# Three key blocks per group, three score slots, one value bank and one product bank in a four-layer attention and convolution kernel

## The chip, the cores and the metric

The kernel runs on one core of a Trainium2 chip. The metric is the device time of one execution in microseconds, as a median of several runs. A core has five engines with a queue each: TensorE (PE in the profile, its weight loads are PEld), VectorE (DVE), ScalarE (ACT), GpSimd (POOL) and SyncE (SP, which only starts DMAs here). Each engine works through its own instructions in their order and waits for the others by semaphores. TensorE writes to PSUM alone, eight banks of 512 fp32 values per partition; VectorE and ScalarE take results out of it.

## The reference

The input x is (4, 256, 48, 48) in fp32; an image is 256 channels by 2304 positions. Four layers follow each other, each as x + layer(group norm of x):

```python
# layer 0: 8 heads of 64, keys and queries of each channel normed over positions
qkv = einsum('oc,bchw->bohw', w_qkv, x); q, k = l2norm(q), l2norm(k)
out = softmax(q^T k * 10) v ; return w_out out + b_out
# layer 1: max pool, blur, four small depthwise convolutions, sigmoid gate, x * gate
# layer 2: one more attention (64 channels, 2304 x 2304) and a batch norm over its output
# layer 3: squeeze-and-excite, 3x3 depthwise convolution, instance norm, leaky ReLU
```

The attention of layer 0 is most of the work: 4 images x 8 heads x 2304 x 2304 scores, and as many weights times values. Layer 2 adds one head per image.

## The kernel before

**Units and groups.** Two heads are worked on together, one in partitions 0 to 63, the other in 64 to 127 (a "pair"; four pairs p=0..3 per image b). A *unit* is 384 queries (`SL`) of one pair against all 2304 keys, which are 18 blocks of 128 (`JB`). A *group* is `G` = 2 blocks, so a unit has `NG` = 9 groups. A *phase* is the 6 units of one pair, 16 phases in all; then four phases of 3 units each are the attention of layer 2.

**One block.** `scores(u, j)` makes two matmuls, one per head, with 64 rows of the array each, into one score slot of two banks (`ps_sc`, two slots), and ScalarE takes the exponential of both (line 229) into a `pt` tile of 128 x 768. `weigh(u, j)` makes two matmuls with 64 columns of the array each (line 242), which add `v` times `pt` into the value bank `av` (`ps_av`, two banks, one in use per unit). In fp32 each matmul is two records in the profile. `add_up(u, g)` adds the `pt` tiles of a group into `acc`: VectorE does it itself (lines 252 and 262) or, for the groups in `PAIRED`, GpSimd adds the two tiles into `half` (line 259) and VectorE adds `half` later (line 255). Per unit that is 13 sums on VectorE and 4 on GpSimd.

**The end of a unit.** `total(u)` sums `acc` over partitions by two matmuls with ones (line 267) into a product bank and takes the reciprocal on VectorE (line 272, 2.56 us). `divide(u)` lets ScalarE check the total (line 279), multiplies `av` by the reciprocal on VectorE (line 282), and checks the reciprocal. Then two output products (line 441), each added to x by VectorE (lines 446 and 450).

**The product banks.** Everything that TensorE makes beside scores, values and convolutions goes to `pj_tile()`, two banks (`ps_pj`): totals, output products, the q, k and v products of the next pair in `project` (lines 397 and 409), products of layer 2, statistics of the norms. A q or k product is copied to SBUF by VectorE (line 401) and then squared in place by ScalarE for its norm (line 402), so its bank is held until both are done; a v product is copied by ScalarE (line 414).

**The order.** `attend` writes the order of TensorE, VectorE, ScalarE and GpSimd out by hand; nothing is moved until the last section. For each group t it issues the scores of t, the sums of t-1, what is due (`finish`), some steps of the phase's *lanes*, a total that is due, and the value products of t-1. Lanes are generators: `project` for the next pair, the group norm, `layer1` for the image before (in p=1 and p=2 of images 1 to 3, and in the first two phases of layer 2), `project2` and `w_stats`. Their steps ("ticks") are spread evenly over the groups of the phase but for the last three. `layer1` is mainly VectorE's: 81 taps over each image and channel half, three to a tick.

**The rest.** Before `attend` the group norm of image 0 and `project(0, ...)` for the first pair run alone ("the first projection"): for six chunks of 384 positions, q, k and v products. The chunks are loaded (line 370) two ahead into three buffers `xs` and scaled by VectorE one ahead (`normed`, line 374); the pair's weights `w` (line 365) have two buffers. All these loads stand in SP's queue. After `attend`, `w_stats` of the last image makes 12 products, each read by VectorE (line 675), and layer 3 follows: `before_conv` with 12 products per image read by ScalarE (line 815), and the convolutions (line 870) in score slots. There a scheduler orders the instructions.

Of the kernel before, what the change touches and what calls it, by code (L numbers as in the profile page):

```python
# [9 lines left out]
F32 = mybir.dt.float32  # L10
AF = mybir.ActivationFunctionType
# [3 lines left out]
P = 128  # L15
# [40 lines left out]
def _drain(gen):  # L56
    for _ in gen:
        pass
# [4 lines left out]

G = 2
NG = JB // G
PAIRED = (1, 3, 5, 7)
NCH = NSL
# [6 lines left out]
def usual_path(  # L74
# [7 lines left out]
    small = ctx.enter_context(tc.tile_pool(name="small", bufs=2))  # L82
    ps_sc = ctx.enter_context(tc.tile_pool(name="ps_sc", bufs=2, space=bass.MemoryType.PSUM))
    ps_av = ctx.enter_context(tc.tile_pool(name="ps_av", bufs=2, space=bass.MemoryType.PSUM))
    ps_pj = ctx.enter_context(tc.tile_pool(name="ps_pj", bufs=2, space=bass.MemoryType.PSUM))

# [121 lines left out]
    big = keep.enter_context(tc.tile_pool(name="big", bufs=2))  # L208
    wqp = main.enter_context(tc.tile_pool(name="wq", bufs=2))
    xsp = main.enter_context(tc.tile_pool(name="xs", bufs=3))  # L210
    op = main.enter_context(tc.tile_pool(name="o", bufs=2))
    ppool = main.enter_context(tc.tile_pool(name="pt", bufs=5))
    apool = main.enter_context(tc.tile_pool(name="acc", bufs=2))
# [33 lines left out]
    def add_up(u, g):  # L247

        pts = [u["pt"][j] for j in range(g * G, (g + 1) * G)]
        if g == 0:  # L250
            u["acc"] = apool.tile([P, 2, SL], F32, tag="acc", name="acc")
            nc.vector.tensor_add(u["acc"], pts[0], pts[1])  # L252
            return
        if u.get("half") is not None:
            nc.vector.tensor_add(u["acc"], u["acc"], u["half"])  # L255
            u["half"] = None
        if g in PAIRED:
            u["half"] = hpool.tile([P, 2, SL], F32, tag="half", name="half")
            nc.gpsimd.tensor_add(u["half"], pts[0], pts[1])  # L259
        else:  # L260
            for pt in pts:
                nc.vector.tensor_add(u["acc"], u["acc"], pt)  # L262

    def total(u):
        u["l"] = pj_tile()
        for h in range(2):
            nc.tensor.matmul(  # L267
                u["l"][h * D : (h + 1) * D, :SL], lhsT=ones, rhs=u["acc"][:, h, :],
                start=True, stop=True,
            )  # L270
        u["rinv"] = rpool.tile([P, SL], F32, tag="rinv", name="rinv")
        nc.vector.reciprocal(u["rinv"], u["l"][:, :SL])  # L272

    finished = {}

    def divide(u):
        i = u["i"]
        junk = rpool.tile([P, SL], F32, tag="junk", name="junk")
        nc.scalar.activation(
            junk, u["l"][:, :SL], AF.Identity, accum_out=checks[:, 0, i : i + 1]  # L280
        )
        nc.vector.tensor_mul(u["o"](), u["av"][:, :SL], u["rinv"])
        finished[u["b"]] = finished.get(u["b"], 0) + 1
        nc.scalar.activation(
            junk, u["rinv"], AF.Identity, accum_out=checks[:, 1, i : i + 1]
        )
# [18 lines left out]
    def attend(phases):  # L305
# [7 lines left out]
        def finish(t):  # L313
            for fn in due.pop(t, ()):
                fn()

        for t, (u, g, st) in enumerate(groups):
            for j in range(g * G, (g + 1) * G):
                scores(u, j)
            if prev is not None:  # L320
                add_up(*prev)
            finish(t)
            if st["gen"] is None:
# [4 lines left out]
            until = -(-st["total"] * st["at"] // (st["n"] - 3))  # L328
            while st["done"] < until and next(st["gen"], st) is not st:
                st["done"] += 1  # L330
            if st["at"] == st["n"] - 1:
                _drain(st["gen"])
            if t in sums:
                total(sums.pop(t))
            if prev is not None:
                pu, pg = prev
                for j in range(pg * G, (pg + 1) * G):
                    weigh(pu, j)
                if pg == NG - 1:
                    sums[t + 1] = pu  # L340
                    due.setdefault(t + 2, []).append(lambda pu=pu: divide(pu))
                    for i, fn in enumerate(pu["after"]):
                        due.setdefault(t + 3 + i, []).append(fn)
            prev = (u, g)
        pu, pg = prev
        add_up(pu, pg)
        for j in range(pg * G, (pg + 1) * G):
            weigh(pu, j)
        for t in sorted(due):
            finish(t)  # L350
# [9 lines left out]
    def project(b, norm, pair):  # L360
# [7 lines left out]
        def fetch(s):  # L368
            xs[s] = xsp.tile([P, NK, SL], F32, tag="xs", name="xs")
            nc.sync.dma_start(xs[s], xv[:, :, b, s * SL : (s + 1) * SL])  # L370
# [8 lines left out]
        fetch(0)  # L379
        fetch(1)  # L380
        q = big.tile([P, N], F32, tag="q", name="q")
# [6 lines left out]
        for s in range(NCH):  # L388
            cols = slice(s * SL, (s + 1) * SL)
            if s + 1 < NCH:  # L390
                normed(s + 1)
            if s + 2 < NCH:
                fetch(s + 2)
            for t, to in ((0, q), (1, kk)):
# [12 lines left out]
            for i in range(SL // P):  # L407
# [7 lines left out]
                v[:, j0 : j0 + SL // P, :].rearrange("p j d -> p (j d)"), ps[:, :SL]  # L415
            )
            yield
        n2 = small.tile([P, 2], F32, tag="n2", name="n2")
# [1331 lines left out]
```

## Time and profile before

| | us |
|---|---|
| median of 3 runs (4351.93 to 4355.94) | 4355.51 |
| the profiled execution | 4356.0 |
| its span, first to last instruction | 4354.3 |
| PE busy (94%) | 4078.9 |
| DVE busy (68%) | 2952.5 |
| ACT busy (43%) | 1857.8 |
| POOL busy (24%) | 1065.0 |
| scores, L223, busy | 1364.9 + 176.6 |
| values, L242, busy | 1322.7 + 192.1 |
| exponentials, L229, busy | 1473.7 |

A row of the timeline gives the start, the time taken, the engine, the line, the operation and its tiles (out<-in), and how many records it merges; in brackets, how long the engine was idle before and what ended that. Matmuls overlap in their pipeline, so a run of them is best measured from its start to the start of the next run. The clock column is the share of TensorE's full clock that was granted; it takes the values 1 and 0.5, and a mean lies between.

### The profile page before, as it was taken

To read this page: it belongs to the slowest core of one execution; us is meant where nothing else is said; L and a number is where in the kernel's file an instruction comes from. 1 tells how busy PE (TensorE), PEld (TensorE's weight loads), DVE (VectorE), ACT (ScalarE), POOL (GpSimd) and SP (SyncE) were. 2 spreads that over 40 slices of the span, in tenths; PEclk is the share of its full clock that TensorE was granted. 3 is DMA by queue.
4 is the path that set the end of the run, shared out by engine and by line. 5 is a ranking of instruction groups with operands and counts; after the bars stand their busy time and mean duration, and the time that the engine had idled before them with its cause. 6 is when DMAs were issued, how large, how long until landed. Compare 5 with 4: busy or idle time off the path is not lost.

```text
span 4354.3 us, 50890 instructions
## 1 busy us (share of the span) xinstructions
PE 4078.9 (94%) x19922; PEld 1805.3 (41%) x19922; DVE 2952.5 (68%) x3719; ACT 1857.8 (43%) x3054; POOL 1065.0 (24%) x632
## 2 busy tenths in 40 slices
PE   7999999999989999999899999998899978899997
PEld 4444444444433344444333444443334433444554
DVE  4555556556989865579898655798975699754222
ACT  3444444444444444444444444444444323343211
POOL 1222222222222322222323222223232221223231
PEclk9999999999999999999999999999999988997999
DMA  4000000000000000000000000000000000000000
GB/s 146 15 15 19 12 15 8 19 15 15 12 11 12 15 12 19 12 15 12 11 15 12 12 19 15 12 15 8 8 1 1 1 1 1 1 1 1 22 33 34
DMA packets 44330, 67.50 MB, mean 16 GB/s; under 512 B 4336, under 2 KB 42032, under 8 KB 42032
## 3 DMA queue, kind: packets, MB, share of 16 engines
q1 hardware_dynamic: 41216, 62.92, 4.7%
q8 instruction: 158, 2.59, 0.3%
q10 hardware_dynamic: 2864, 1.24, 0.1%
q14 instruction: 92, 0.75, 0.1%
HBM read 54.71 MB, written 9.44 MB: 15 GB/s over the span
## 4 chain that ended last, share of the span: by engine, by line
PE 68%; DVE 27%; issue 2%; ACT 2%; POOL 1%; DMA 0%; DVEq 0%; ACTq 0%; POOLq 0%
PE sc L223 24%; PE av L242 23%; DVE acc L262 7%; DVE l1acc L564 7%; PE sc L870 7%; PE pj L397 5%; PE pj L441 3%; PE pj L409 2%; DVE acc L255 2%; DVE rinv L272 2%; PE pj L267 1%; PE pj L663 1%; ACT pt L229 1%; DVE xs L374 1%; PE pj L641 1%
## 5 line engine op out<-in xcount | busy, mean ns | idle before, releaser
L229 ACT ACTIVATE pt<-sc 128x768 f32<-128x768 f32 x1944 | 1473.7, 808 | 1524.1 <-PE sc L223 1429.3
L259 POOL TENSOR_TENSOR half<-pt 128x768 f32<-128x768 f32 x432 | 852.7, 1974 | 2630.6 <-ACT pt L229 2317.2
L223 PE MATMUL sc<-q,k 64*128 64x384 f32 x6912 | 1364.9, 513 | 52.2 <-ACT pt L229 49.4
L242 PE MATMUL av<-pt,v 128*64 128x384 f32 x6912 | 1322.7, 503 | 0.0
L262 DVE TENSOR_TENSOR acc<-acc,pt 128x768 f32<-128x768 f32 x864 | 947.8, 1097 | 128.0 <-ACT pt L229 42.2
L223 PEld LDWEIGHTS sc<-q,k 64*128 64x128 f32 x6912 | 596.5, 187 | 811.3 <-ACT pt L229 304.9
L242 PEld LDWEIGHTS av<-pt,v 128*64 128x64 f32 x6912 | 433.5, 137 | 726.2 <-issue 714.4
L255 DVE TENSOR_TENSOR acc<-acc,half 128x768 f32<-128x768 f32 x432 | 416.4, 964 | 192.0 <-POOL half L259 191.2
L564 DVE SCALAR_TENSOR_TENSOR l1acc<-pd,grid,l1acc 128x256 f32<-128x256 f32 x640 | 347.2, 542 | 18.2
L272 DVE RECIPROCAL rinv<-pj 128x384 f32<-128x384 f32 x108 | 275.9, 2555 | 110.7 <-PE pj L267 110.6
L397 PE MATMUL pj<-xs,w 128*128 128x384 f32 x768 | 303.1, 520 | 40.2 <-issue 32.7
L870 PE MATMUL sc<-pad,diag 128*128 128x384 f32 x864 | 293.0, 499 | 4.5 <-ACT pad L851 4.5
L402 ACT ACTIVATE pj<-pj 128x384 f32<-128x384 f32 x192 | 91.2, 475 | 402.6 <-DVE q L401 266.1
L870 PEld LDWEIGHTS sc<-pad,diag 128*128 128x128 f32 x864 | 165.8, 194 | 130.0 <-issue 16.0
L397 PEld LDWEIGHTS pj<-xs,w 128*128 128x128 f32 x768 | 136.2, 193 | 186.0 <-issue 101.5
L441 PE MATMUL pj<-o,wo 128*128 128x384 f32 x384 | 175.8, 540 | 39.2 <-DVE x L450 16.5
L450 DVE TENSOR_TENSOR x<-pj,x 128x384 f32<-128x384 f32 x144 | 79.9, 555 | 170.1 <-PE pj L441 170.1
L223 PE MATMUL sc<-qv,kd 64*128 64x384 f32 x864 | 176.6, 527 | 19.1 <-ACT pt L229 19.1
L242 PE MATMUL av<-pt,qv 128*64 128x384 f32 x864 | 192.1, 534 | 0.0
L409 PE MATMUL pj<-w,xs 128*128 128x128 f32 x1152 | 152.8, 283 | 13.7 <-DVE x L450 12.2
L409 PEld LDWEIGHTS pj<-w,xs 128*128 128x128 f32 x1152 | 139.2, 193 | 60.2 <-issue 28.9
L252 DVE TENSOR_TENSOR acc<-pt 128x768 f32<-128x768 f32 x108 | 107.1, 992 | 45.4 <-ACT pt L229 45.1
(137 smaller groups left out, 2102.4 us busy)
## 6 DMA issues: line engine op xcount, KB each, us to landing
xs<-in_x_dram SPq DMA_DIRECT2D x96, 384.0 KB, 3.3
x<-in_x_dram SPq DMA_DIRECT2D x8, 1152.0 KB, 8.6
out_dram<-x SPq DMA_DIRECT2D x8, 1152.0 KB, 4.2
w<-in_wqkv_dram SPq DMA_DIRECT2D x32, 192.0 KB, 3.7
wo<-in_wout_dram ACTq DMA_DIRECT2D x1, 512.0 KB, 4.8
dw<-in_dww_dram ACTq DMA_DIRECT2D x1, 132.0 KB, 5.4
wph<-in_thphi_w_dram ACTq DMA_DIRECT2D x2, 64.0 KB, 4.6
Ww<-in_W_w_dram ACTq DMA_DIRECT2D x2, 64.0 KB, 5.3
```

The costliest lines, as they stand in the source:

```text
L223: nc.tensor.matmul(ps[:, h, :SL], lhsT=u["of"]["k"][r, j * P : (j + 1) * P], rhs=u["of"]["q"][r, u["qc"]], start=True, stop=True,)
L229: nc.scalar.activation(pt, ps[:, :, :SL], AF.Exp)
L242: nc.tensor.matmul(u["av"][r, :SL], lhsT=value(u, j, h), rhs=pt[:, h, :], start=j == 0, stop=j == JB - 1,)
L255: nc.vector.tensor_add(u["acc"], u["acc"], u["half"])
L259: nc.gpsimd.tensor_add(u["half"], pts[0], pts[1])
L262: nc.vector.tensor_add(u["acc"], u["acc"], pt)
L272: nc.vector.reciprocal(u["rinv"], u["l"][:, :SL])
L397: nc.tensor.matmul(ps[:, :SL], lhsT=w[:, k, t, :], rhs=xs[s][:, k, :], start=k == 0, stop=k == NK - 1,)
L409: nc.tensor.matmul(ps[:, i * P : (i + 1) * P], lhsT=xs[s][:, k, i * P : (i + 1) * P], rhs=w[:, k, 2, :], start=k == 0, stop=k == NK - 1,)
L441: nc.tensor.matmul(ps[:, :SL], lhsT=wo[:, p, k * P : (k + 1) * P], rhs=o, start=True, stop=True)
L564: nc.vector.scalar_tensor_tensor(acc, src, w, acc, ALU.mult, ALU.add)
L870: nc.tensor.matmul(ps[:, h, :SL].rearrange("p (r c) -> p r c", c=HW), lhsT=diag[:, k, t, :], rhs=pad[:, r0 + dr : r0 + dr + RS, dc : dc + HW],
```

## The change

Groups are three blocks (`G = 3`, six groups a unit); PSUM is cut as three score slots (six banks), one value bank and one product bank; `pt` has seven buffers instead of five. GpSimd adds the first two blocks of groups 1 to 4, and VectorE adds the third block of these groups and the older `half`. A new function `take` copies the value bank to SBUF on ScalarE as soon as the last value product of a unit is issued, and `divide` reads this copy. The check of the total moves from `divide` to `total`. In `attend`, a group gives the place ahead of its value products either to what is due or to one step of the lanes; other steps due in the group come after its value products. `project` has one weight buffer instead of two, two chunk buffers instead of three, loads one chunk ahead, and scales a chunk after the products of the one before it.

```diff
-G = 2
+G = 3
-PAIRED = (1, 3, 5, 7)
+PAIRED = (1, 2, 3, 4)
...
-    ps_sc = ctx.enter_context(tc.tile_pool(name="ps_sc", bufs=2, space=bass.MemoryType.PSUM))
-    ps_av = ctx.enter_context(tc.tile_pool(name="ps_av", bufs=2, space=bass.MemoryType.PSUM))
-    ps_pj = ctx.enter_context(tc.tile_pool(name="ps_pj", bufs=2, space=bass.MemoryType.PSUM))
+    ps_sc = ctx.enter_context(tc.tile_pool(name="ps_sc", bufs=3, space=bass.MemoryType.PSUM))
+    ps_av = ctx.enter_context(tc.tile_pool(name="ps_av", bufs=1, space=bass.MemoryType.PSUM))
+    ps_pj = ctx.enter_context(tc.tile_pool(name="ps_pj", bufs=1, space=bass.MemoryType.PSUM))
...
-    wqp = main.enter_context(tc.tile_pool(name="wq", bufs=2))
-    xsp = main.enter_context(tc.tile_pool(name="xs", bufs=3))
+    wqp = main.enter_context(tc.tile_pool(name="wq", bufs=1))
+    xsp = main.enter_context(tc.tile_pool(name="xs", bufs=2))
-    ppool = main.enter_context(tc.tile_pool(name="pt", bufs=5))
+    ppool = main.enter_context(tc.tile_pool(name="pt", bufs=7))
...
         pts = [u["pt"][j] for j in range(g * G, (g + 1) * G)]
+        half = u.pop("half", None)
+        if g in PAIRED:
+            u["half"] = hpool.tile([P, 2, SL], F32, tag="half", name="half")
+            nc.gpsimd.tensor_add(u["half"], pts[0], pts[1])
+            pts = pts[2:]
         if g == 0:
             u["acc"] = apool.tile([P, 2, SL], F32, tag="acc", name="acc")
             nc.vector.tensor_add(u["acc"], pts[0], pts[1])
-            return
-        if u.get("half") is not None:
-            nc.vector.tensor_add(u["acc"], u["acc"], u["half"])
-            u["half"] = None
-        if g in PAIRED:
-            u["half"] = hpool.tile([P, 2, SL], F32, tag="half", name="half")
-            nc.gpsimd.tensor_add(u["half"], pts[0], pts[1])
-        else:
-            for pt in pts:
-                nc.vector.tensor_add(u["acc"], u["acc"], pt)
+            pts = pts[2:]
+        if half is not None:
+            nc.vector.tensor_add(u["acc"], u["acc"], half)
+        for pt in pts:
+            nc.vector.tensor_add(u["acc"], u["acc"], pt)
...
         nc.vector.reciprocal(u["rinv"], u["l"][:, :SL])
+        i = u["i"]
+        junk = rpool.tile([P, SL], F32, tag="junk", name="junk")
+        nc.scalar.activation(
+            junk, u["l"][:, :SL], AF.Identity, accum_out=checks[:, 0, i : i + 1]
+        )
+
+    def take(u):
+        u["araw"] = rpool.tile([P, SL], F32, tag="araw", name="araw")
+        nc.scalar.copy(u["araw"], u["av"][:, :SL])
...
-        nc.scalar.activation(
-            junk, u["l"][:, :SL], AF.Identity, accum_out=checks[:, 0, i : i + 1]
-        )
-        nc.vector.tensor_mul(u["o"](), u["av"][:, :SL], u["rinv"])
+        nc.vector.tensor_mul(u["o"](), u["araw"], u["rinv"])
...
             if prev is not None:
                 add_up(*prev)
-            finish(t)
...
-            while st["done"] < until and next(st["gen"], st) is not st:
+            if t in due:
+                finish(t)
+            elif st["done"] < until and next(st["gen"], st) is not st:
                 st["done"] += 1
-            if st["at"] == st["n"] - 1:
-                _drain(st["gen"])
             if t in sums:
                 total(sums.pop(t))
...
                 if pg == NG - 1:
+                    take(pu)
                     sums[t + 1] = pu
...
+            while st["done"] < until and next(st["gen"], st) is not st:
+                st["done"] += 1
+            if st["at"] == st["n"] - 1:
+                _drain(st["gen"])
             prev = (u, g)
...
         fetch(0)
-        fetch(1)
...
             if s + 1 < NCH:
-                normed(s + 1)
-            if s + 2 < NCH:
-                fetch(s + 2)
+                fetch(s + 1)
...
+            if s + 1 < NCH:
+                normed(s + 1)
             yield
```

More of the change, by code (lines that the diff above doesn't have):

```diff
@@ L272, in total @@
         nc.vector.reciprocal(u["rinv"], u["l"][:, :SL])
-    finished = {}
-    def divide(u):
         i = u["i"]
@@ L281, in divide @@
         )
-        nc.vector.tensor_mul(u["o"](), u["av"][:, :SL], u["rinv"])
+    def take(u):
+        u["araw"] = rpool.tile([P, SL], F32, tag="araw", name="araw")
+        nc.scalar.copy(u["araw"], u["av"][:, :SL])
+    finished = {}
+    def divide(u):
+        i = u["i"]
+        junk = rpool.tile([P, SL], F32, tag="junk", name="junk")
+        nc.vector.tensor_mul(u["o"](), u["araw"], u["rinv"])
         finished[u["b"]] = finished.get(u["b"], 0) + 1
@@ L348, in attend @@
             weigh(pu, j)
+        take(pu)
         for t in sorted(due):
```

## The prediction

> **What bounds the kernel now.** I read the slices of the page first, then the timeline of TensorE alone in a calm stretch, then the busy times stage by stage, then single places in the timeline. The slices of the page:
>
> ```profile
> PE   7999999999989999999899999998899978899997
> DVE  4555556556989865579898655798975699754222
> PEclk9999999999999999999999999999999988997999
> ```
>
> TensorE is full nearly everywhere, but VectorE is full too in three double humps and once near the end. Those are the phases whose lanes carry `layer1`. Counting exponentials (108 to a phase of one head pair) gives the borders of the phases; busy times in some of them, columns length, PE, PEld, DVE, ACT, POOL, clock:
>
> ```profile
> 848.30:1047.80 199.50, 198.64 (x1034) 85.59 (x1032) 116.37 (x132) 98.00 (x163) 44.74 (x25) 1.00 0.05 15
> 1047.80:1274.70 226.90, 210.09 (x1046) 88.66 (x1044) 202.13 (x256) 102.64 (x177) 61.86 (x33) 0.96 0.05 13
> 1274.70:1509.70 235.00, 206.74 (x1032) 87.41 (x1030) 209.55 (x260) 102.63 (x176) 66.03 (x31) 0.96 0.05 13
> 3584.20:3752.60 168.40, 135.65 (x590) 61.30 (x588) 154.77 (x220) 50.17 (x80) 39.67 (x21) 0.85 0.00 1
> 3752.60:3868.40 115.80, 115.00 (x590) 52.81 (x588) 69.69 (x88) 44.14 (x67) 21.80 (x12) 1.00 0.00 1
> 3962.00:3975.00 13.00, 12.97 (x22) 5.90 (x22) 7.33 (x15) 0.62 (x2) 8.38 (x25) 0.50 0.00 0
> ```
>
> So ten head-pair phases (all of image 0, p=0 and p=3 of the others) last 197 to 200 us and are TensorE's, DVE 58%. Six (p=1, 2 of images 1 to 3) last 226 to 235 us with DVE 89% busy (202 of 227, 210 of 235) and TensorE no longer full: VectorE's. Of the four phases of the second attention, the first two (157 and 168 us) are VectorE's, the last two TensorE's. TensorE in a calm stretch:
>
> ```profile
> 1038.00 1.56 PE L223 MATMUL sc<-q,k 64*128 64x384 f32 x8
> 1039.49 1.51 PE L242 MATMUL av<-pt,v 128*64 128x384 f32 x8
> 1040.93 1.56 PE L223 MATMUL sc<-q,k 64*128 64x384 f32 x8
> 1042.42 1.51 PE L242 MATMUL av<-pt,v 128*64 128x384 f32 x8
> ```
>
> A score run of two blocks takes 1.49 us, a value run 1.44. In a value run the weight loads start 0.32 us apart, four steps, 1.29 us. The rest, 0.20 and 0.15 us, is paid at each change between the two shapes. This rebuilds a calm phase: 54 x 1.49 + 54 x 1.44 + 12 q/k products x 1.49 + 6 v products x 1.53 + 12 output products x 0.8 + 6 totals x 0.70 = 199 us, against 199.5.
>
> **What the Trainium skill says.** "TensorEngine Tiling (Array Packing)", Key Properties: changing the tiling mode drains the array. The trace agrees, with 0.35 us for a there and back. "TensorE: Matmul & The Clock Gate", Part 1: the clock is halved unless the array has been busy. The trace agrees, and adds that TensorE may be 99.8% busy (12.97 of 13.00 us, last row above) with 64-row products and stay at 0.50. "SBUF — State Buffer", Who interferes with whom: a VectorE instruction with two SBUF inputs and a GpSimd one that reads SBUF exclude each other. The trace agrees: below, two sums that take 2.02 us elsewhere take 3.43 beside a GpSimd sum, 1.41 lost.
>
> ```profile
> 1058.09 3.43 DVE L262 TENSOR_TENSOR acc<-acc,pt 128x768 f32<-128x768 f32 x2
> 1058.79 1.92 POOL L259 TENSOR_TENSOR half<-pt 128x768 f32<-128x768 f32 x1 [4.64 <-ACT pt L229]
> ```
>
> **The change, part by part.** The sum is made against the profiled execution, 4356.0 us (span 4354.3), 0.5 over the median of the runs.
>
> *Three blocks to a group.* A unit has 6 groups instead of 9, so 3 x 0.35 = 1.05 us less. 108 units would give 113 us. It counts only where TensorE sets the pace: 10 phases x 6 units x 1.05 = 63 us, and 6 units in the last two phases, 6.3 us. In VectorE's phases 0. VectorE's 13 sums and GpSimd's 4 in a unit stay as many. Inside a gap, output and projection products no longer follow each other (4 per phase, 0.09 us each, a shape change saved): 4 us back. The third score slot only makes room for three blocks; TensorE's idle at L223 is 52 us in all.
>
> *One bank for all products (`pj`).* A product must now wait until its forerunner is evacuated. The turn, from the prologue:
>
> ```profile
> 37.13 2.75 PE L397 MATMUL pj<-xs,w 128*128 128x384 f32 x8
> 38.62 0.56 DVE L401 COPY q<-pj 128x384 f32<-128x384 f32 x1 [2.41 <-PE pj L397]
> 39.27 0.47 ACT L402 ACTIVATE pj<-pj 128x384 f32<-128x384 f32 x1 [1.47 <-DVE q L401]
> 39.66 0.19 ACT L402 ACTIVATION_READ_ACCUMULATOR pj<-pj 128x1 f32 x1
> 39.91 1.60 PE L409 MATMUL pj<-w,xs 128*128 128x128 f32 x12
> ```
>
> q starts at 37.13 (its records are the first four of eight), is copied, squared in place, and its bank is free at 39.85: 2.8 to 2.9 us, where the product alone holds TensorE 1.49, so 1.36 lost if another follows at once. A v product: 39.91 to its copy at 41.55, 0.48, so 2.17, 0.64 lost. A product that VectorE alone evacuates: 1.49 + 0.56 + 0.05, 0.61 lost. In the order of the changed program a run of values (6 x 0.32 + 0.15 = 2.09 us) or of scores stands between most products, which covers the 1.36. Uncovered in TensorE's ten phases: q or k directly ahead of a total 14 times, v 9 times, second-attention products 4 times: 19 + 6 + 2 = 27 us. Net there: -63 + 4 + 27 = **-32 us**. The last two phases: 10 adjacent products x 0.61, and three totals with one value run before the next product (reciprocal 2.56, check 0.7, wait 0.3, less 2.09: 1.4 each), against -6.3: **+4**.
>
> *The same bank in VectorE's phases.* There TensorE waits at the bank until VectorE comes, and VectorE then has nothing queued if the next evacuation follows in its own order. In a head-pair phase the order shows four such places: q ahead of a total (square 0.7, total 0.7, latency 0.3: 1.7), a total ahead of k (check 0.7, product 1.7: 2.4), an output sum ahead of q (1.7), statistics (about 1): 7 us, less 1.5 in the stretches where TensorE leads. **+33** for six. None of this is in the trace of before: bounds -1.5 (all covered by `layer1` steps) and +12 a phase. For the second attention's two phases, some 3 and 6 places of 1 to 2.4 us: **+14**, bounds 0 and +28.
>
> *The first projection*, drained alone before any attention. Before: 20.46 (first product) to 49.58 (last square), 29.1 us for six chunks. After, each chunk is q, k, v in turn on one bank. At full clock 2 x 2.85 + 2.17 = 7.9 us, in all 5 x 7.9 + 5.7 = 45, +16. But the stage starts cold: the first loads are 0.64 us apart, and it became warm at 26 us after 5.5 us without a break. With breaks after every product TensorE works 2.6 of 4.2 us, so I take cold: q or k turn 4.2, v 3.8 (twice 0.128 a record, then 0.19, 0.48, 0.05), 5 x 12.2 + 8.4 = 69. **+40**, lower bound +16. Loads: one chunk ahead instead of two, 8 to 12 us for a load of 3.3 (page, part 6), hidden; if the x loads delay them, up to 5 us.
>
> *The end.* The 12 products for the statistics run 1.28 us apart (half clock); on one bank each takes 1.68 (product to evacuation) + 0.57 + 0.05 = 2.30: 11 x 1.02. The 12 before the first convolution, 1.25 apart: 1.75 + 0.67 + 0.05 = 2.47: 11 x 1.22. In the convolutions the order splits the remaining products into about 15 more insertions x 0.35. **+29**, bounds +10 (clock recovers) and +40.
>
> *At nothing.* `take`: 108 ScalarE copies x 0.48 = 52 us on an engine 49% busy in a calm phase (98 of 199.5). It waits for the last value product; behind it stand the next exponentials, which wait for scores later than that anyway. If ScalarE were late, the next value run has 2.1 us of scores ahead of it; the cover gone costs at most 0.5 x 108 us. The check of the total now waits on ScalarE behind the reciprocal, ahead of one group's exponentials, by some 0.5 us; the score slots absorb it. The product in `divide` now reads SBUF only: 0 to -0.1 us x 108, taken as 0. One weight buffer: the load (3.7 us) has over a group, 4.2 us, and the SP queue holds only the chunk load behind it.
>
> **Sum**: -32 + 4 + 33 + 14 + 40 + 29 = +88, **4444 us**.
>
> **The rivals.** (a) Milder: the prologue warms (-24) and the `layer1` steps cover VectorE's waits in its eight phases (-37): 4383. For it: the two are my least certain terms. Against: the listed places have nothing between them. Chance 0.22. (b) Worse: VectorE and TensorE fall into lockstep at the bank, 15 us instead of 6 a phase in eight phases: 4516. For it: the reciprocal holds the only bank 3.3 us in every unit. Chance 0.14. (c) **Faster**: GpSimd's sums collide less with VectorE. Place: the eight VectorE phases; price 1.42 us for each collision (sums of 1232 ns mean there, 958 in a calm phase), some 21 in a phase, 170 in all. Half of them gone is -120: 4324. It decides from 62 collisions (8 a phase) on, where 88 us are paid. For it: the GpSimd sum now waits for VectorE's use of the half before it, which could put it beside PSUM reads. Against: right behind that use VectorE has another two-input sum. Chance 0.10. (d) The terms cancel: 0.04. That the runs don't get longer is excluded: the order shows six matmuls in each.
>
> **The numbers.** Forecast 0.50, the rest as given. The range takes in (a) and most of (b): 4375 to 4505. About 0.2% (9 us) is what a measurement can tell from no change: faster 0.10, same 0.05, slower 0.85.
>
> **What would show it.** Score runs of 2.13 us and value runs of 2.09; calm phases of 196 to 197 us; first exponential at 93 us (69 if warm) instead of 53; VectorE phases of 230 to 242 us with new idle time of VectorE ahead of reciprocals and q/k copies; 2.3 us between the last products. I am wrong if VectorE's phases shrink, or if calm phases are longer than 199.5.

## The result and the profile after

The changed kernel takes 4419.61 us (median of four runs, 4415.05 to 4423.38) against 4354.71 us before: 1.0149 times the time, 95% interval 1.0132 to 1.0167. It is slower, by less than the 4444 forecast and well inside the range. The profiled execution took 4415.05 us with a span of 4413.3, so 59.0 us of span are to be placed.

The slices of the page after hardly differ from before:

```profile
PE   6999999999888999998889999988899867997997
DVE  3565566556888856578887555788865788562222
PEclk9999999999999999999999999999999878996999
```

The first slice is thinner (a longer first projection), and VectorE's humps are 8s where they had 9s: it is less full in phases that are as long as before. Stage by stage (columns as before: length, PE, PEld, DVE, ACT, POOL, clock, and the DMA share and rate):

```profile
853.60:1049.90 196.30, 193.14 (x1034) 88.39 (x1032) 115.75 (x132) 97.64 (x168) 56.20 (x25) 1.00 0.05 15
1049.90:1276.60 226.70, 201.45 (x1040) 92.27 (x1038) 190.63 (x255) 102.59 (x182) 66.66 (x32) 0.96 0.05 13
1276.60:1513.40 236.80, 204.46 (x1038) 92.99 (x1036) 199.84 (x260) 102.30 (x183) 73.04 (x33) 0.94 0.04 12
3580.90:3769.20 188.30, 136.91 (x594) 64.32 (x592) 153.48 (x222) 50.67 (x84) 47.12 (x23) 0.83 0.00 1
3980.00:4413.30 433.30, 375.96 (x1040) 195.26 (x1034) 110.58 (x206) 74.81 (x90) 111.31 (x99) 0.87 0.05 22
```

Row 1 is a calm phase, 3.2 us shorter. Rows 2 and 3 are VectorE's phases: their lengths are those of before (226.9 and 235.0) to within 2 us, but VectorE's busy time fell from 202.13 to 190.63 and from 209.55 to 199.84. Some 10 us of busy time went away and 11 us of idle time came. Row 4, the second phase of the second attention, is 19.9 us longer with the same work: all of it is idle time of VectorE. Row 5 is the end, 36.6 longer.

The runs of matmuls in the same calm phase, TensorE alone:

```profile
1039.70 2.21 PE L223 MATMUL sc<-q,k 64*128 64x384 f32 x12
1041.83 0.91 PE L451 MATMUL pj<-o,wo 128*128 128x384 f32 x2
1042.68 2.16 PE L242 MATMUL av<-pt,v 128*64 128x384 f32 x12
1044.76 2.21 PE L223 MATMUL sc<-q,k 64*128 64x384 f32 x12
```

Twelve records in place of eight: a score run lasts 2.13 us from start to start, a value run 2.08. The runs did get longer. The terms of the forecast beside what the trace shows:

| term | forecast | measured |
|---|---|---|
| ten phases that TensorE paces | -32 | -27.9 |
| VectorE's six phases of the first attention | +33 | +7.0 |
| first two phases of the second attention | +14 | 0.0 and +19.9 |
| its last two phases | +4 | +6.9 and -1.1 |
| first projection | +40 | +17.5 |
| the end | +29 | +36.6 |
| sum | +88 | +58.9 |

Two terms were much too large, and the question is why: did the bank cost VectorE's phases nothing, or did something give it back?

### The profile page after: what moved, and what is told of

It reads as the page before. It is cut to its first block, busy times and chain, and to the rows that moved or that the text cites. A ratio compares the mean times of both kernels' runs of the same rounds, so it can differ in the third digit from the quotient of the medians.

```text
span 4413.3 us, 51038 instructions
## 1 busy us (share of the span) xinstructions
PE 4010.0 (91%) x19922; PEld 1868.3 (42%) x19922; DVE 2889.6 (65%) x3719; ACT 1856.7 (42%) x3162; POOL 1228.9 (28%) x632
## 3 DMA queue, kind: packets, MB, share of 16 engines
q8 instruction: 158, 2.59, 0.2%
## 4 chain that ended last, share of the span: by engine, by line
PE 69%; DVE 25%; ACT 2%; issue 2%; POOL 2%; DMA 0%; DVEq 0%; ACTq 0%; POOLq 0%
PE sc L223 23%; PE av L242 22%; DVE l1acc L574 7%; PE sc L880 7%; PE pj L405 6%; DVE acc L262 5%; PE pj L451 3%; PE pj L417 3%; DVE acc L260 2%; DVE rinv L272 2%; PE pj L673 2%; PE pj L267 2%; POOL half L253 1%; DVE acc L257 1%; PE pj L651 1%
## 5 line engine op out<-in xcount | busy, mean ns | idle before, releaser
L229 ACT ACTIVATE pt<-sc 128x768 f32<-128x768 f32 x1944 | 1438.0, 811 | 806.5 <-PE sc L223 742.8
L253 POOL TENSOR_TENSOR half<-pt 128x768 f32<-128x768 f32 x432 | 1019.2, 2359 | 2419.0 <-DVE acc L260 1401.3
L223 PE MATMUL sc<-q,k 64*128 64x384 f32 x6912 | 1289.3, 506 | 17.6 <-ACT pt L229 16.1
L242 PE MATMUL av<-pt,v 128*64 128x384 f32 x6912 | 1249.7, 496 | 0.0
L262 DVE TENSOR_TENSOR acc<-acc,pt 128x768 f32<-128x768 f32 x864 | 886.9, 1027 | 97.8 <-ACT pt L229 23.8
L223 PEld LDWEIGHTS sc<-q,k 64*128 64x128 f32 x6912 | 625.7, 189 | 634.8 <-issue 272.9
L260 DVE TENSOR_TENSOR acc<-acc,half 128x768 f32<-128x768 f32 x432 | 415.0, 961 | 99.8 <-POOL half L253 98.9
L574 DVE SCALAR_TENSOR_TENSOR l1acc<-pd,grid,l1acc 128x256 f32<-128x256 f32 x640 | 380.7, 595 | 18.4
L275 ACT ACTIVATE junk<-pj 128x384 f32<-128x384 f32 x108 | 53.0, 491 | 431.9 <-DVE rinv L272 431.9
L409 DVE COPY q<-pj 128x384 f32<-128x384 f32 x96 | 53.4, 557 | 209.2 <-PE pj L405 209.2
L267 PE MATMUL pj<-acc,ones 128*64 128x384 f32 x432 | 99.0, 538 | 89.7 <-ACT pj L410 58.5
```

What stands on the lines that cost most here:

```text
L223: nc.tensor.matmul(ps[:, h, :SL], lhsT=u["of"]["k"][r, j * P : (j + 1) * P], rhs=u["of"]["q"][r, u["qc"]], start=True, stop=True,)
L229: nc.scalar.activation(pt, ps[:, :, :SL], AF.Exp)
L242: nc.tensor.matmul(u["av"][r, :SL], lhsT=value(u, j, h), rhs=pt[:, h, :], start=j == 0, stop=j == JB - 1,)
L260: nc.vector.tensor_add(u["acc"], u["acc"], half)
L574: nc.vector.scalar_tensor_tensor(acc, src, w, acc, ALU.mult, ALU.add)
```

## Experiments

All stage times come from one profiled execution each, with the borders at the same exponentials; stages of the same code differ by up to some 3 us between executions, in the second attention above all, where three phases together differ by 7.2 (467.7 after and 474.9 in run 1, the same code there). Edits shift the line numbers by a few. "Calm" is the sum of the ten phases of the first attention that TensorE paces, "VectorE's" that of the other six, "L2" the first three phases of the second attention, "rest" its last phase and the end.

| kernel | first projection | calm | VectorE's | L2 | rest | span |
|---|---|---|---|---|---|---|
| before | 53.4 | 1989.8 | 1384.3 | 440.9 | 485.9 | 4354.3 |
| after | 70.9 | 1961.9 | 1391.3 | 467.7 | 521.4 | 4413.3 |
| 1 two banks at the ends | 54.2 | 1961.5 | 1390.6 | 474.9 | 486.4 | 4367.5 |
| 2 no step at the total | 70.9 | 1941.8 | 1349.9 | 463.4 | 519.5 | 4345.5 |
| 3 two slots, three banks | 52.6 | 2153.7 | 1446.6 | 457.3 | 479.7 | 4590.0 |
| 4 before, one bank | 76.4 | 2061.2 | 1501.6 | 470.6 | 524.6 | 4634.5 |
| 5 second half buffer | 76.4 | 1960.9 | 1393.1 | 472.3 | 520.3 | 4423.0 |
| 6 after, no GpSimd sums | 73.8 | 1957.8 | 1376.1 | 467.4 | 519.9 | 4394.7 |
| 7 before, no GpSimd sums | 52.8 | 2000.4 | 1291.6 | 427.1 | 484.3 | 4256.2 |
| 8 both mends (1 and 2) | 54.5 | 1941.8 | 1350.5 | 463.5 | 485.5 | 4295.8 |
| 9 as 6, square from the copy | 63.6 | 1948.6 | 1372.9 | 467.9 | 519.9 | 4372.9 |
| 10 as 6, no step at the total | 70.9 | 1942.0 | 1341.7 | 458.6 | 518.3 | 4331.5 |
| 11 before, GpSimd in calm phases | 53.4 | 1990.0 | 1297.2 | 425.7 | 486.3 | 4252.6 |
| 12 change with mends | 53.3 | 1938.1 | 1350.0 | 460.4 | 485.4 | 4287.3 |

**1. Two banks at both ends.** Outside `attend` the value bank is free, so products there take it in turn with the product bank.

```diff
+    ends = {"on": True, "n": 0}
+
     def pj_tile():
+        if ends["on"]:
+            ends["n"] += 1
+            if ends["n"] % 2:
+                return ps_av.tile([P, 512], F32, tag="av", name="av")
...
+    ends["on"] = False
     attend(phases)
+    ends["on"] = True
```

> The changed kernel, but outside attention (first projection, second statistics, convolutions), where the value bank lies unused, products take the product bank and the value bank in turn. Theory (the single bank's turn is the whole cost of both ends): the first projection comes back from 70.9 to 53-55 us and the end from 433 to 397-405, all phases between unchanged within 1 us each, in all 4415 - 17.5 - 33 = 4365. Rival (the order of the new loop costs the ends: one chunk loaded ahead instead of two and norms after the products, and the split remaining products in the convolutions): the ends stay long, first projection 62 or more, end 420 or more, 4395 to 4415.

Measured: 4368.83 us, 1.0033 times before (1.0019 to 1.0048). The first projection is back to 54.2 us, last phase and end to 486.4 (before 485.9). The end alone takes 398.5 us (before 396.7). So the single bank's turn is the whole loss at both ends to within 2 us, which leaves next to nothing for the shallower loading and the new loop there. The products for the statistics, first in the changed kernel:

```profile
3983.94 1.65 PE L673 MATMUL pj<-y,Ww 64*128 64x384 f32 x2 [3.27 <-ACT junk L275]
3986.24 1.64 PE L673 MATMUL pj<-y,Ww 64*128 64x384 f32 x2 [0.66 <-DVE bst L685]
```

then with two banks:

```profile
3976.09 1.48 PE L679 MATMUL av<-y,Ww 64*128 64x384 f32 x2
3977.37 1.48 PE L679 MATMUL pj<-y,Ww 64*128 64x384 f32 x2
```

One bank: 2.30 us from product to product, with a wait of 0.66 for VectorE each time. Two banks: 1.28, no wait.

**2. No lane step in the group that holds a total.** The steps due there are taken in the unit's other five groups, so that no product stands next to a total.

```diff
-            elif st["done"] < until and next(st["gen"], st) is not st:
+            elif t not in sums and st["done"] < until and next(st["gen"], st) is not st:
                 st["done"] += 1
-            if t in sums:
+            summed = t in sums
+            if summed:
                 total(sums.pop(t))
...
-            while st["done"] < until and next(st["gen"], st) is not st:
+            while not summed and st["done"] < until and next(st["gen"], st) is not st:
                 st["done"] += 1
```

> The changed kernel, but in the one group of six that holds the total no lane step is taken (its share falls to the next groups), so no product stands next to a total. Theory (uncovered turns of the one bank cost some 27 us in TensorE's ten phases, and part of the 26 us in the second attention): calm phases shorter by 1.5 to 3 us each, the second attention's four phases shorter by 5 to 20 together, VectorE's phases within 2, in all 4415 - 25 - 12 = 4378 (4360 to 4395). Rival (the work that is pushed into five groups stands next to other products there, two steps in a gap, and waits for the bank just as long): 4410 to 4425, calm phases unchanged.

Measured: 4352.13 us, 0.9995 times before (0.9986 to 1.0004), more gain than expected. Calm phases fall by 20.1 in all, as forecast for uncovered turns. But VectorE's six phases fall by 41.4, where I expected next to nothing: the bank may have cost a good deal there after all, and the +7.0 of the table above would then be a balance. (The edit moves steps of `layer1` away from the total too, so that this run alone does not show that it was the bank.)

**3. Two score slots and three product banks.**

```diff
-    ps_sc = ctx.enter_context(tc.tile_pool(name="ps_sc", bufs=3, space=bass.MemoryType.PSUM))
+    ps_sc = ctx.enter_context(tc.tile_pool(name="ps_sc", bufs=2, space=bass.MemoryType.PSUM))
...
-    ps_pj = ctx.enter_context(tc.tile_pool(name="ps_pj", bufs=1, space=bass.MemoryType.PSUM))
+    ps_pj = ctx.enter_context(tc.tile_pool(name="ps_pj", bufs=3, space=bass.MemoryType.PSUM))
```

> The changed kernel, but two score slots and three product banks in place of three and one (value bank still one). Theory (the bank's turn costs both ends and the uncovered turns; the third slot is needed by three blocks): first projection 53-56 us, end 397-405, no wait of TensorE at the product bank; but the third score block of a group waits for the first exponential, some 0.3 to 0.6 us in each of 36 groups, so calm phases 206 to 216 us instead of 196; VectorE's phases 225 to 237; in all 4360 + 100 = 4460 (4400 to 4510). Rival (the third slot matters little, as TensorE's idle at the score line was 52 us in all before): calm phases 193 to 197 us, in all 4290 to 4340, faster than before.

Measured: 4593.23 us, 1.0554 times before (1.0537 to 1.0572). The ends are cured, but a calm phase takes 216.0 us, 19.6 more than after: 0.54 for each of its 36 groups. The waits of TensorE in a calm phase are one single line (total us, times, longest):

```profile
PE sc L223 <- ACT pt L229: 13.2, 36, 0.5
```

The third score block waits for the first exponential, once in every group. (These waits are 13.2 of the 19.6 us; the rest, 6.4, the waits do not show.) Three blocks need the third slot, and its two banks are what the products lost. The whole run is 83 us above the end of the range I expected: most calm phases lie at its edge (216), and VectorE's phases, at 239 to 245 us, above the 225 to 237 I had put down.

**4. The kernel before with one product bank.** Two blocks to a group as before; the check of the total moves into `total`, as in the change.

```diff
-    ps_pj = ctx.enter_context(tc.tile_pool(name="ps_pj", bufs=2, space=bass.MemoryType.PSUM))
+    ps_pj = ctx.enter_context(tc.tile_pool(name="ps_pj", bufs=1, space=bass.MemoryType.PSUM))
...
         nc.vector.reciprocal(u["rinv"], u["l"][:, :SL])
+        i = u["i"]
+        junk = rpool.tile([P, SL], F32, tag="junk", name="junk")
+        nc.scalar.activation(
+            junk, u["l"][:, :SL], AF.Identity, accum_out=checks[:, 0, i : i + 1]
+        )
...
```

> The kernel before (two blocks to a group, two score slots, two value banks) with one product bank instead of two; the check of the total moved to right behind the reciprocal as in the change, since it must be done before the bank is asked for again. Theory (the single bank costs both ends some 54 us, and costs TensorE's and VectorE's phases on its own, with no gain from longer runs): first projection +16 to +40, end +30 to +40, calm phases +2 to +6 each, since runs of two blocks (1.49 us) cover less of a turn of 1.36 to 2.4 us, second attention +25 to +60, VectorE's phases +1 to +10 each; in all 4355 + 130 = 4485 (4440 to 4540). Rival (in attention the one bank costs next to nothing and the loss is at the ends alone): 4405 to 4420. The same run tells whether VectorE's collisions with GpSimd fall with the bank alone (theory: yes, from 21-24 to about 15 in a VectorE phase) or with three blocks to a group (then they stay).

Measured: 4636.42 us, 1.065 times before (1.0632 to 1.0668), 150 us beyond what I expected. Calm phases lose 71 us in all, VectorE's 117. One of the latter:

```profile
1351.40:1606.10 254.70, 218.07 (x1034) 91.37 (x1032) 208.52 (x260) 101.93 (x176) 61.16 (x31) 0.91 0.04 12
```

VectorE's busy time is that of before (209.55); its idle time went from 25.5 to 46.2 us. So one bank, with the check moved, costs such a phase some 20 us. The second question of this run has a clear answer too. Taking for each VectorE instruction what it takes above the median of its kind, the excess in these phases is 28 to 33 us here and 29 to 35 before, but 19 to 24 after. If that excess is taken for collisions with GpSimd, they do not fall with the bank; they fall with the rest of the change, the new groups and their order of sums.

**5. A second buffer for GpSimd's half sum.** In the changed kernel a GpSimd sum and the VectorE sums around it stand like this:

```profile
1105.85 0.95 DVE L260 TENSOR_TENSOR acc<-acc,half 128x768 f32<-128x768 f32 x1
...
1106.90 0.96 DVE L262 TENSOR_TENSOR acc<-acc,pt 128x768 f32<-128x768 f32 x1
1106.94 2.59 POOL L253 TENSOR_TENSOR half<-pt 128x768 f32<-128x768 f32 x1 [2.71 <-DVE acc L260]
```

VectorE's use of the old half releases GpSimd 0.04 us after VectorE has begun its next sum. VectorE's sum takes its usual 0.96 us, GpSimd's 2.59 instead of 1.81. "SBUF — State Buffer", section "SBUF: two separate sides" of the Trainium skill, says that of the two the one that starts first holds the port for its whole instruction; the trace agrees. Before, it was VectorE that came second. I took this order for the cause of the missing +26 and undid it:

```diff
-    hpool = main.enter_context(tc.tile_pool(name="half", bufs=1))
+    hpool = main.enter_context(tc.tile_pool(name="half", bufs=2))
```

> The changed kernel with a second buffer for GpSimd's half sum, nothing else. Theory (in the changed order a GpSimd sum is released by VectorE's use of the half before it, so it begins just behind a VectorE sum that is already running, and GpSimd pays for the collision; that is why VectorE's phases grew 1.2 us each and not 5.5): with a second buffer GpSimd starts at its exponentials again, its sum takes 2.0 to 2.2 us instead of 2.44 to 2.49, VectorE's lost time in collisions goes back from 19-24 to 29-35 us a phase, and VectorE's six phases of the first attention get longer by 7 to 12 us each; calm phases unchanged; in all 4415 + 60 + 5 = 4480 (4450 to 4500). Rival (collisions fell because VectorE, waiting for the bank, is less often busy when GpSimd works): collisions and phases stay, 4410 to 4420.

Measured: 4426.23 us, 1.0169 times before (1.0152 to 1.0186). GpSimd in a phase of p=2, first after, then here (count; busy us, mean ns; idle before, by releaser):

```profile
L253 POOL TENSOR_TENSOR half<-pt 128x768 f32<-128x768 f32 x24 | 59.8, 2493 | 122.8 <-DVE acc L260 66.1 <-ACT pt L229 56.6
```

```profile
L253 POOL TENSOR_TENSOR half<-pt 128x768 f32<-128x768 f32 x23 | 51.3, 2235 | 119.8 <-ACT pt L229 101.3 <-DVE acc L260 18.5
```

The mechanism is there: GpSimd is released by the exponentials again, its sum is shorter, and VectorE's excess rises from 19 to 21.5 us (p=1) and from 23.5 to 29.5 (p=2). But the time did not follow: VectorE's six phases are 1.8 us longer together, not 42 to 72 (p=2 by 5.0, p=1 shorter by 3.2), while its idle time in the first phase of p=2 fell from 37.0 to 30.1 us. (Of the 9.7 us more in the span, 5.5 are in the first projection, see below, and 4.6 in the second attention, within the scatter there.) As an explanation of the time my theory fell: in the changed kernel, time that VectorE loses to GpSimd comes out of its waits, at least the 2 to 6 us a phase that this run adds.

**6 and 7. No GpSimd sums, with and without the change.** If collisions and bank hide each other, both have to be seen alone. VectorE makes all sums, 24 more in a phase.

```diff
-PAIRED = (1, 2, 3, 4)
+PAIRED = ()
```

(7 sets the same in the kernel before.)

> The changed kernel with all sums of exponentials on VectorE (24 more sums of 0.96 us in a phase), none on GpSimd, so no collisions. Theory (the bank costs VectorE's phases some 11 us each, which falling collisions hid): VectorE's phases 235 to 243 us; beside the next run, which is the same without the change, 8 to 14 us longer each; in all 4415 + 6 x 6 = 4450 (4430 to 4480). Rival (the bank costs VectorE's phases next to nothing): 226 to 230 us, no longer than in the next run by more than 2.

> The kernel before with all sums of exponentials on VectorE, none on GpSimd. VectorE's load is then 210.7 - 29.7 + 24 x 0.96 = 204 us and 219 - 34.5 + 23 = 207 us in its two kinds of phase, idle 22: phases of 224 to 231 us, calm phases 199 to 200; in all 4355 - 6 x 3 = 4337 (4315 to 4365). Both theories expect the same here; it is what the run before it is held against.

Measured, one execution each: 4396.71 and 4257.98 us. The same two VectorE phases with the change:

```profile
1050.90:1274.50 223.60, 202.87 (x1038) 93.30 (x1036) 195.38 (x278) 102.78 (x183) 10.62 (x9) 0.95 0.05 13
1274.50:1509.80 235.30, 204.01 (x1038) 93.02 (x1036) 203.07 (x285) 102.46 (x182) 10.82 (x7) 0.94 0.05 13
```

and without it:

```profile
1055.40:1269.30 213.90, 201.82 (x1038) 86.76 (x1036) 196.65 (x279) 102.92 (x176) 10.78 (x9) 0.98 0.05 14
1269.30:1485.10 215.80, 202.09 (x1038) 86.46 (x1036) 198.97 (x284) 102.45 (x176) 10.97 (x7) 0.98 0.05 14
```

Nearly the same work, but VectorE idles 28.2 and 32.2 us with one bank, 17.3 and 16.8 with two. Over the six phases the change costs 1376.1 - 1291.6 = **84.5 us** when no collisions cover it; 75.8 of them are idle time of VectorE. The waits tell which: summed over these phases, VectorE waits 58.0 us for q and k products (12.9 without the change) and 15.3 us for totals (4.8), and TensorE waits 125.4 us for the bank, behind the check, the sums into x or the squares, against 1.2 us behind a sum into x with two banks. The granted clock falls with these waits (0.95 and 0.94 in the rows, 0.98 without the change); how much of the 84.5 the slower products are is not separated.

GpSimd's sums cost the kernel before 1384.3 - 1291.6 = 92.7 us there, and the changed kernel only 1391.3 - 1376.1 = 15.2. 84.5 - 92.7 + 15.2 = 7.0; this holds by construction and is no check of its own, but it gives the sizes of the two terms behind the +7.0. The rival of run 6 is wrong, and the size in my theory (8 to 14 a phase) holds in p=1 (9 to 10) and is too small in p=2 (16 to 20).

In all, run 6 lies 53 us below what I had expected: its phases did not grow to 235 to 243 us. Run 7 lies 80 us below what I had expected, because I had added up durations of VectorE that overlap in part (208.6 us summed in the first phase, 196.65 busy) and taken its idle time as given, which fell from 25 to 17 us; only its calm phases are longer than before, by 10.6 us in all. A surprise beside it: in run 7, VectorE does 24 more sums in each of these phases and is *less* busy than before (198.97 against 209.55), since each GpSimd sum saved it one sum of 0.96 us (23 in a phase) and the excess over the usual durations was 29 to 35. Over the six phases this fall of the busy time is about half of the 92.7 us; the other half, 45.1, is idle time that went with the sums, and I have not taken it apart.

**8. Both mends.** The edits of 1 and 2 together.

> The changed kernel with both mends: two banks in turn outside attention, and no lane step in the group that holds the total. Theory (the costs lie in different places and add up): 4352 - 46 = 4306 (4300 to 4315), 1.1% faster than the kernel before. Rival (they share a cause): 4325 or more.

Measured: 4297.09 us, 0.9871 times before (0.9854 to 0.9887), 9 us better than expected. The two costs lie in different places and add up. Three blocks with one bank can beat the kernel before, if the bank is not asked for twice in a row.

**9 and 10. Which turns of the bank cost VectorE's phases?** Both start from run 6. 9 reads the squares from the copy in SBUF, so that a q or k product gives its bank back at VectorE's copy; 10 adds the edit of run 2.

```diff
+                junk = rpool.tile([P, SL], F32, tag="junk", name="junk")
                 nc.scalar.activation(
-                    ps[:, :SL], ps[:, :SL], AF.Square, accum_out=ss[:, t, s : s + 1]
+                    junk, to[:, cols], AF.Square, accum_out=ss[:, t, s : s + 1]
                 )
```

> The changed kernel without GpSimd sums (as the earlier run of that, 4396.7 us), and the squares of q and k read from the copies in SBUF instead of from the bank, so that a q or k product's turn of the bank ends at VectorE's copy, some 0.75 us earlier; 12 turns in a phase. Theory (VectorE's phases are paced by turns of the bank, of every kind): first projection shorter by about 8 us, VectorE's phases by 4 to 9 each, calm phases by 0 to 3, in all 4396.7 - 8 - 40 - 10 = 4340 (4320 to 4360). Rival (the turns that cost time there are those of the total, which holds the bank over the reciprocal and the check, and of the sums into x): VectorE's phases within 2 of 223.6 and 235.3, in all 4380 to 4390.

> The changed kernel without GpSimd sums (4396.7 us) and with no lane step in the group that holds the total. Theory (a good part of the 84 us that the bank costs VectorE's six phases comes from products next to a total): the phases of p=1 shorter by 2 to 5 us, those of p=2 by 8 to 12, calm phases by 2 each, in all 4396.7 - 40 - 20 - 6 = 4330 (4315 to 4350). Rival (the turns of q, k and the sums into x among themselves set them): VectorE's phases within 2 of the run without the mend, in all 4365 to 4380.

Measured, one execution each: 4374.85 and 4333.34 us. The shorter q and k turns take 10 us from the first projection (some 2.7 of it the clock, see below) and 9 from the calm phases, but only 3.2 from VectorE's six: my theory of "every turn" falls, the rival holds. Keeping steps away from the total takes 34.4, of which 28.9 in p=2 (10.0, 11.1, 7.8). TensorE's waits for the bank in the first phase of p=2, behind the check of the total and behind sums into x (total us, times, longest), first in run 6, then in run 10:

```profile
PE pj L417 <- ACT junk L275: 6.0, 1, 6.0
PE pj L405 <- ACT junk L275: 4.4, 1, 4.4
PE pj L405 <- DVE x L460: 3.4, 1, 3.4
```

```profile
PE pj L418 <- ACT junk L275: 0.2, 1, 0.2
PE pj L418 <- DVE x L461: 4.9, 2, 4.4
PE pj L406 <- DVE x L461: 3.9, 2, 3.5
```

In run 6 a v product waited 6.0 us until the check of the total had let go of the bank. In run 10 that is gone: 10.4 us behind the check fell to 0.2 in this phase, which is 10.0 us shorter, and 53.5 to 0.5 over all six. What is left is behind VectorE's sums into x (75.5 us over the six phases) and the squares (19.4). The remaining 1341.7 - 1291.6 = 50.1 us I have not taken apart by a run; that the bank, held until VectorE comes to these sums in its queue, is their cause is read from the waits only.

**11 and 12. Each scheme at the best found here.** Since GpSimd's sums help only where TensorE sets the pace, they stay there and go elsewhere.

```diff
-        if g in PAIRED:
+        if g in PAIRED and u["gp"]:
...
+        u["gp"] = b == 0 or p in (0, 3)
         return u
...
-            "b": ("l2", b),
+            "b": ("l2", b), "gp": b >= 2,
```

11 is the kernel before with this edit, 12 the change with this, both mends and the square from the copy.

> The kernel before, with GpSimd's sums left only in the phases that TensorE paces; in VectorE's eight phases VectorE makes them. Theory (in VectorE's phases the collisions cost the kernel before 13 to 19 us each; in calm phases the GpSimd sums save up to 3): the run without any GpSimd sums, 4258, less some 12 to 30 in the calm phases: 4240 (4225 to 4255). Rival (its gain came from elsewhere than VectorE's phases): above 4260.

> The changed kernel with two banks in turn outside attention, no step at the total, GpSimd's sums only in the phases that TensorE paces, and squares read from the copies. It is held against the run before it: three blocks with one bank against two blocks with two, each at its best here. Theory (calm phases are 5 us better with three blocks, VectorE's still 3 to 10 us worse for the bank): 4297 - 40 - 15 = 4242 (4225 to 4265), within 20 of the run before it. Rival (without the collisions the bank's cost comes out in full in VectorE's phases): 4270 or more, clearly behind it.

Measured: 11 takes 4251.47 us, as expected, **0.9768** times before (0.9755 to 0.9781); 12 takes 4289.00, 0.9851 (0.9836 to 0.9867). Three blocks are 51.9 us better in the calm phases (1938.1 against 1990.0), 52.8 worse in VectorE's and 34.7 worse in the second attention. The rival of run 12 was right: without collisions to hide it, the bank's cost comes out. Beside run 8, which has GpSimd's sums in every phase, run 12's six phases of VectorE are no shorter (1350.5 and 1350.0): with three blocks and one bank, taking these sums away gains nothing there. The best kernel found has two blocks, two banks, and fewer GpSimd sums.

## Why the forecast came out as it did

**Longer runs, -32: right.** The calm phases gave 27.9. Of the forecast's 27 us of uncovered turns in them, 25 stood at a total; run 2, which moves those products, gets back 20.1.

**VectorE's six phases, +33: the failed step.** The forecast said that "VectorE then has nothing queued" at four places, 5.5 us a phase. The waits exist, but the term was wrong twice. What the change costs there when GpSimd makes no sums is 84.5 us, 14 a phase, above the upper bound I gave (12). I had counted four places with one turn each; run 10 shows that steps next to a total alone cost 34.4 us. That the other 50.1 are the bank's too is read from TensorE's waits, not shown by a run. And what the change takes away was in the forecast only as rival (c), at 0.10: collisions with GpSimd. It was half right. Excess over the usual durations fell by 10 to 11 us a phase, of the 29 to 35. But (c) would have it that time follows collisions, and after the change it doesn't (run 5). GpSimd's sums cost 77.5 us less with the change; how much of that is fewer collisions and how much is collisions falling into time in which VectorE waits for a product anyway is not separated. I call shown that the two large terms cancel (6 and 7), that the bank alone does not lower the collisions (4), and that in the changed kernel raising them again by a part costs nearly nothing (5). That two errors of this size met is luck: without the 77.5 us the result would have been 4497, 53 us above the forecast instead of 24 below it.

**The second attention, +18: right in sign, too small.** Measured +25.7. Its second phase has the +19.9, without GpSimd sums +24.9 (187.8 against 162.9). TensorE's longest waits there are at products for which the bank is held until VectorE comes, so I take it for the bank again; no run shows it alone:

```profile
PE pj L673 <- DVE qv L655: 9.4, 3, 7.4
PE pj L267 <- DVE kd L631: 7.8, 2, 4.7
```

**The first projection, +40: mechanism right, the clock wrong.** The turns were as worked out: cold 4.2 to 4.3 us for q, warm 2.88 (forecast 2.8 to 2.9, though its own lines give only 2.72 from the start of q to the end of its square). The step "With breaks after every product [...] so I take cold" failed. TensorE after, then the same code in run 5:

```profile
20.36 2.93 PE L405 MATMUL pj<-xs,w 128*128 128x384 f32 x4 [1.74 <-DVE xs L385]
24.55 1.56 PE L405 MATMUL pj<-xs,w 128*128 128x384 f32 x4 [1.26 <-ACT pj L410]
27.43 1.60 PE L417 MATMUL pj<-w,xs 128*128 128x128 f32 x12 [1.33 <-ACT pj L410]
```

```profile
36.63 2.93 PE L405 MATMUL pj<-xs,w 128*128 128x384 f32 x4 [1.33 <-ACT pj L410]
40.88 1.60 PE L417 MATMUL pj<-w,xs 128*128 128x128 f32 x12 [1.32 <-ACT pj L410]
```

2.93 us for a product is the half clock, 1.56 the full one; the clock column, 1.00 in this stage, does not show it, since the trace's first entry of the clock is the change to full, at 23.3 us after and at 39.8 us in run 5. After, only the first product was cold; in run 5 the first five were. Run 5 became warm, and both stayed so, in spite of breaks of 1.3 us after a q or k product. The lower bound of the forecast, +16 at full clock, was the right value.

**The end, +29: right, a little small.** The 12 statistics products came 2.30 us apart and the 12 before the first convolution 2.47, both as forecast, which makes 24.6 us. Two of the latter:

```profile
4022.27 1.65 PE L673 MATMUL pj<-y,Ww 64*128 64x384 f32 x2 [0.82 <-ACT tmp L825]
4024.74 1.65 PE L673 MATMUL pj<-y,Ww 64*128 64x384 f32 x2 [0.82 <-ACT tmp L825]
```

The other 12, where I had 5, lie in the rest; run 1 shows that they belong to the bank as well, since it brings the end back to within 1.8 us.

**At nothing.** The shallower loads cost nothing that shows outside the attention: run 1 has them, and its first projection is 0.8 us longer than before. The copy in `take` and the single weight buffer lie inside the attention, where no run takes them out alone; the calm phases of run 12 are 51.7 us below before, of the 59 that the forecast gave to longer runs, which leaves them little.

**The rivals.** (a) was right that the first projection gets warm, and near the mark for VectorE's phases of the first attention, but not for its reason: their waits were not covered by `layer1` steps. The range, said to take in most of (b), ended at 4505, below the 4516 of (b).

## What to carry to other kernels

A bank is not free when its product ends, but when the last reader has let go: count for each product the time from its start to its last evacuation, and look in the order for two such products with less than that between them. Where two engines pace a phase together, a removed loss and a new wait can cancel and leave nothing in the time, so put each at zero in turn (here by taking GpSimd's sums out of both kernels) before calling either small. Work given to GpSimd can cost VectorE more than it saves: compare VectorE's busy time with and without it, not the number of its instructions.

## What the runs showed of the hardware that I had not expected

- TensorE's change to full clock is not fixed by the code. The first projection is the same code in the changed kernel and in runs 5 and 6, and took 70.9, 76.4 and 73.8 us, since one, five and three of its products ran at half clock. "TensorE: Matmul & The Clock Gate", Part 1, of the Trainium skill says that the window in which activity is judged runs freely, about 3.4 us long, so that the count of cold products varies from run to run; this agrees, and shows that products of 2.93 us with breaks of 1.3 us can be enough to become warm. Beside it, the stretch of 64-row products in the forecast was 99.8% busy by the profile (12.97 of 13.00 us) and stayed at 0.50, so that busy time as the profile counts it does not settle the clock here.
- 24 sums fewer on VectorE in a phase made it busier: 209.55 us with GpSimd's sums, 198.97 without.
- Of two sums that start 0.04 us apart on VectorE and GpSimd, the second alone paid: 2.59 us in place of 1.81.
